# A two-layer transformer on one core: layer 1's attention weights loaded and padded when row 3's slot begins, in the tiles in which rows were prepared

## The chip, the core and the metric

The kernel runs on one core of a Trainium2 chip. A core has a matrix engine (TensorE, "PE" in the profile, its weight loads "PEld"), a vector engine (VectorE, "DVE"), an engine for activation functions (ScalarE, "ACT"), a general engine (GpSimd, "POOL") and a queue engine (SyncE, "SP") that issues most of the transfers. Each engine works through its own list of instructions in order and waits on semaphores for the others. The metric is the time of one execution in microseconds of device time; lower is better.

## The reference, cut to what matters

The input x is 4 rows (batch entries) of 512 tokens with 128 channels, all in 32-bit floats. Two layers are computed, each as x = x + attention(norm(x)) + experts(norm(x)):

```python
# layer 0: a window of 64 tokens per token and head, and 16 gated experts (best 4)
strain = disp_win - disp[:, :, :, None, :]
bond_logits = gelu(strain @ W_strain + rel_emb @ W_pos) @ W_bond
damage = sigmoid(gelu(strain @ W_dmg + b_dmg) @ W_dmg_out + b_dmg_out)
weights = softmax(where(mask, bond_logits - 10.0 * damage, -inf))
# layer 1: full attention with 16 heads of 8 channels, and 8 relu experts (best 2)
q, k, v = split(xn @ w_qkv, 3)
attn = softmax(q @ k.T / sqrt(128)) @ v @ w_out
```

What the change touches is `w_qkv`, a matrix of 128 x 384 that gives layer 1's queries, keys and values.

## The kernel before, in words

The rows go through layer 0 one after the other, in the loop `for b in range(B)` (L731). In row b's slot four kinds of work are woven together step by step (`weave`): the band logits of row b (`band_logits`, L555: VectorE subtracts shifted projections into tiles `z`, L572, ScalarE puts them through Gelu, L574 and L578, TensorE sums them, L586); the gated experts of row b (`gated_experts`, L659); the band values of row b-1 (`band_values`, L305 on); and layer 1's relu experts of earlier rows (`relu_experts`, L399, whose two products are L388 and L454, with a relu on ScalarE, L396, and an addition on POOL, L459). In the second half of a slot the next row is also prepared (`prepare`, L504): normalised into tile `xn`, transposed into `xnT`, and scaled by its root mean square in tile `sq`.

At the end of a row's band logits the exponentials `e` are formed from the logits on VectorE (L628), taken on ScalarE (L632) and stored to memory as `by_t` (L633). The band values read them back in another order, into tiles `f` (L312), transpose them on TensorE (L321), copy them to `g` (L322), store them as `by_s` (L327) and read them as `wb` (L339) for the products with the values (L353).

After the loop, layer 0's pools are closed and layer 1's are opened in their place. `full_attention` runs for all four rows, woven with the band values of row 3 and the remaining relu experts. Its order on TensorE is written out by hand: a list of steps, in each of which products of scores (L935) for maxima (L952, VectorE) and for exponentials (L959, ScalarE) alternate, chained so that they stay in this order, and the experts' products are chained behind them. Everything else is ordered ahead of time by a planner: it takes the instructions in the order of the program, or ahead of it by 4000 where the code says so, and places each when its inputs should be ready.

Queries and keys are made for groups of four heads. `w_qkv` holds 8 columns a head; a product needs each head at 32 columns, so the weights are first spread into `wqk`: POOL clears it (L765) and VectorE copies the 8 columns of each head into it, once for the queries and once for the keys (L767). A group's queries are a product into the bank `abank` (L823) and a copy to tile `q` on ScalarE (L827); its keys are L832 and L836, and go through the same bank. The values are L811, and L815 copies them into `vaug`.

Tiles lie in pools, which are stacked in each partition's memory in the order in which they are opened: `keep`, `small`, `chain`, `wp`, and then for layer 0 `prep` (xn, xnT, sq and wdT, one buffer each), `hold0`, `zp` (four tiles of 8,192 bytes a partition, which hold the `z` and also the `e`), `lp`, `ap`, `fp`. For layer 1 the pools `work` (q, k, the results of attention), `one` (w_qkv, w_out, wqk, vaug, nmax) and `ep` (exponentials) take the place of layer 0's, from where `prep` began. `nmax` is cleared by POOL (L777) before VectorE writes maxima into it, and `vaug` likewise (L775, L776).

Of the kernel before, what the change touches and what calls it, by code (L numbers as in the profile page):

```python
# [22 lines left out]
FP = mybir.dt.float32  # L23
# [6 lines left out]
B, T, C = 4, 512, 128  # L30
# [49 lines left out]
def woven(*tracks):  # L80


    live = [[g, n, 0] for g, n in tracks]
    while live:
        t = min(live, key=lambda v: (v[2] + 1) / v[1])
        t[2] += 1
        if next(t[0], "end") == "end" or t[2] == t[1]:
            live.remove(t)
        yield


def weave(*tracks):
    for _ in woven(*tracks):
        pass
# [3 lines left out]
def two_layers(ctx: ExitStack, tc: tile.TileContext, w: dict, consts: bass.AP, out: bass.AP):  # L98
    nc = tc.nc
# [7 lines left out]
    def bank():  # L107
        return ps_f.tile([P, 512], FP, tag="f", name="bank")
# [16 lines left out]
    def c_(name):  # L125
        return cst[:, offs[name][0]:offs[name][1]]
# [80 lines left out]
    def layernorm(b, dst, pin=False):  # L207

        mv = small.tile([P, TPB, 2], FP, tag="mv", name="mv")
        for i in range(TPB):  # L210
            st = small.tile([P, 6], FP, tag="st", name="st")
            ins = nc.vector.bn_stats(st, x1[:, b * TPB + i, :])
            if pin and not i:
                tc.keep_in_program_order(ins)
            nc.vector.bn_aggr(mv[:, i, :], st)
        rs = inv_sqrt(mv[:, :, 1], 1.0)
        for i in range(TPB):
            nc.vector.tensor_scalar(
                dst[:, i, :], x1[:, b * TPB + i, :], mv[:, i, 0:1], rs[:, i:i + 1],
                ALU.subtract, ALU.mult,  # L220
            )

    def inv_sqrt(src, scale):

        sd = small.tile([P, TPB], FP, tag="sd", name="sd")
        nc.scalar.activation(sd, src, AF.Sqrt, bias=eps, scale=scale)
        rs = small.tile([P, TPB], FP, tag="rs", name="rs")
        nc.vector.reciprocal(rs, sd)
        return rs

    def transposed(src):

        pt = bank()
        for i in range(TPB):
            nc.tensor.transpose(pt[:, i * P:(i + 1) * P], src[:, i, :], ident)
        return pt
# [44 lines left out]
    def add_rows(b, py):  # L281
        nc.vector.tensor_tensor(rows_of(b), rows_of(b), py, ALU.add)


    chain = ctx.enter_context(tc.tile_pool(name="chain", bufs=2))
    wp = ctx.enter_context(tc.tile_pool(name="wp", bufs=2))
    xT = keep.tile([C, B * T], FP, name="xT")


# [178 lines left out]


    with ExitStack() as l0:  # L470
        prep = l0.enter_context(tc.tile_pool(name="prep", bufs=1))
        hold = l0.enter_context(tc.tile_pool(name="hold0", bufs=2))
        zp = l0.enter_context(tc.tile_pool(name="zp", bufs=4))
        lp = l0.enter_context(tc.tile_pool(name="lp", bufs=1))
# [29 lines left out]
        def prepare(b):  # L504

            xn = prep.tile([P, TPB, C], FP, tag="xn", name="xn")
            layernorm(b, xn, b > 0)
            pt = transposed(xn)
            xnT = prep.tile([C, T], FP, tag="xnT", name="xnT")
            nc.scalar.copy(xnT, pt)  # L510
            yield
            proj = hold.tile([P, 2, 2, PADW], FP, tag="proj", name="proj")
            nc.gpsimd.memset(proj[:, :, :, 0:4], 0.0)
            for kind in (1, 0):
                for hg in range(2):
                    pp = bank()
                    nc.tensor.matmul(pp, merged[:, kind, hg, :], xnT, start=True, stop=True)
                    nc.scalar.copy(proj[:, kind, hg, 4:4 + T], pp)
            ready[b] = [proj]
            yield  # L520
            sq = prep.tile([P, TPB, C], FP, tag="sq", name="sq")
            nc.vector.tensor_tensor(sq, xn, xn, ALU.mult)
            ss = small.tile([P, TPB], FP, tag="ss", name="ss")
            nc.vector.tensor_reduce(ss, sq, AX.X, ALU.add)
            rr = inv_sqrt(ss, 1.0 / C)
            for i in range(TPB):
                nc.vector.tensor_scalar_mul(sq[:, i, :], xn[:, i, :], rr[:, i:i + 1])

            xb = x1[:, b * TPB:(b + 1) * TPB, :]
            nc.vector.tensor_tensor(xb, xb, xn, ALU.add)  # L530
            yield
            pt = transposed(sq)
            tT = hold.tile([C, T], FP, tag="tT", name="tT")
            nc.scalar.activation(tT, pt, AF.Identity, scale=scale0)
            pv = bank()
            for i in range(TPB):
                nc.tensor.matmul(pv[:, i * P:(i + 1) * P], xnT[:, i * P:(i + 1) * P], w_val, start=True, stop=True)
            valn = chain.tile([P, TPB, C], FP, tag="valn", name="valn")
            nc.scalar.copy(valn.rearrange("p t c -> p (t c)"), pv)
            pg = bank()  # L540
            for i in range(TPB):
                nc.tensor.matmul(pg[:, i * E0:(i + 1) * E0], tT[:, i * P:(i + 1) * P], gate_wT, start=True, stop=True)
            scores = small.tile([P, TPB, E0], FP, tag="scores0", name="scores0")
            nc.vector.tensor_tensor(
                scores, pg[:, :TPB * E0].rearrange("p (t e) -> p t e", e=E0),
                gate_b[:, None, :].to_broadcast([P, TPB, E0]), ALU.add,
            )
            yield
            route = small.tile([P, TPB, E0], FP, tag="route0", name="route0")
            routes(zp, "z", scores, E0, K0, c_("lt16"), route)  # L550
            rT = route_rows(hold, route, E0, route_d[0][b], LIMIT + 1.0)
            ready[b] += [valn, tT, rT]
            yield
# [105 lines left out]
        def gated_experts(b):  # L659
# [40 lines left out]
            finish(*late)  # L700
            add_rows(b, ya)

        preparation = prepare(0)
        for _ in range(2):
            next(preparation)
# [25 lines left out]
        for b in range(B):  # L731
            logits_b, gated_b = band_logits(b), gated_experts(b)
            if not b:
                weave((logits_b, 6), (preparation, 4))
            first = [(logits_b, 30 if b else 24), (gated_b, 7)]
            second = [(logits_b, 37), (gated_b, 10)]
            if b:
                first.append((band_values(b - 1, ready[b - 1][1]), 23))
                experts[b - 1] = relu_experts(b - 1)
                second.append((experts[b - 1], 22))  # L740
            if b > 1:
                first.append((experts[b - 2], 22))
            if b + 1 < B:
                second.append((prepare(b + 1), 6))
            weave(*first)
            weave(*second)
# [4 lines left out]
    one = ctx1.enter_context(tc.tile_pool(name="one", bufs=1))  # L751
# [4 lines left out]
    def abank():  # L756
        return ps_a.tile([P, T], FP, tag="a", name="abank")

    w_qkv = one.tile([C, 3 * C], FP, name="w_qkv")
    nc.sync.dma_start(out=w_qkv, in_=w["L1_attn_w_qkv"])  # L760
    w_out = one.tile([C, C], FP, name="w_out")
    nc.sync.dma_start(out=w_out, in_=w["L1_attn_w_out"])

    wqk = one.tile([C, 2, 4, 4, 32], FP, name="wqk")
    nc.gpsimd.memset(wqk, 0.0)  # L765
    for s in range(2):
        nc.vector.tensor_copy(  # L767
            wqk[:, s, :, :, 0:8].rearrange("c g h e -> c (g h) e"),
            w_qkv[:, s * C:(s + 1) * C].rearrange("c (h e) -> c h e", e=8),
        )  # L770

    vaug = [one.tile([P, TPB, H, 32], FP, name=f"vaug{i}") for i in range(2)]
    nmax = [one.tile([P, TPB, 4, 32], FP, name=f"nmax{i}") for i in range(2)]
# [8 lines left out]
    def full_attention():  # L782
# [37 lines left out]
        def queries(n):  # L820
            b, g = groups[n]
            pq = abank()
            nc.tensor.matmul(  # L823
                pq, wqk[:, 0, g].rearrange("c h e -> c (h e)"), xT[:, b * T:(b + 1) * T], start=True, stop=True
            )
            q[n] = work.tile([P, T], FP, tag="q", name="q")
            nc.scalar.copy(q[n], pq)  # L827

        def keys(n):
            b, g = groups[n]  # L830
            pk = abank()
            nc.tensor.matmul(  # L832
                pk, wqk[:, 1, g].rearrange("c h e -> c (h e)"), xT[:, b * T:(b + 1) * T], start=True, stop=True
            )
            k[n] = work.tile([P, T], FP, tag="k", name="k", bufs=3)
            nc.scalar.activation(k[n], pk, AF.Identity, bias=c_("ones8"))  # L836
# [72 lines left out]
        for n, (b, g) in enumerate(groups):  # L909
            t = m_step[8 * n]  # L910
# [7 lines left out]
            t = x_step[8 * n + 7]  # L918
# [87 lines left out]
```

## Time and profile before

| what | us |
|---|---|
| three runs | 1360.2, 1353.03, 1360.58 |
| their median | 1360.2 |
| the profiled execution's own time | 1354.64 |
| its span, first to last instruction | 1352.8 |
| busy: TensorE, VectorE, ScalarE, POOL | 1165.9, 1007.9, 1018.8, 87.3 |
| row 3's slot of layer 0, about | 693 to 917 |
| first score product of layer 1 (L935) | 933.13 |

The profile is one execution. Its rows give busy time, which is not the same as time on the path: an engine that is idle may cost nothing, and a short step may hold up everything. The chain of work that ended last is followed back from the last instruction, at each step to what released it. Timelines give the start, the length, the engine, the line and what ended the idle time ahead of an instruction. Windows give the busy time of each engine in a stretch, with the clock that TensorE was granted (1.00 is full) and how busy the transfer engines were.

### The profile page before, as it was taken

Reading aid. Unit: us, or ns where it says so; the run is one execution under the profiler, and the core shown is the slowest. Engines: PE = TensorE matmul, PEld = TensorE weight load, DVE = VectorE, ACT = ScalarE, POOL = GpSimd, SP = SyncE. Lnnn points to the kernel's source line nnn. Section 1 sums busy time; section 2 is a strip of 40 time slices with the busy share of each in tenths; the row PEclk is TensorE's granted clock in tenths of the full one; section 3 lists DMA queues with packets and bytes.
Section 4 is the critical chain, followed back from the end, with each engine's and each line's share of the span. In section 5 each row is a group of like instructions: output and inputs, shape, how many; then the busy total and the mean of one; then the engine's idle time right before and its main releaser. Section 6 shows DMA issues by size and latency. Waiting matters only on the chain. (4 is left out here: it accounts for less than half of the span.)

```text
span 1352.8 us, 17415 instructions
## 1 busy us (share of the span) xinstructions
PE 1165.9 (86%) x6763; PEld 448.1 (33%) x6763; DVE 1007.9 (75%) x1085; ACT 1018.8 (75%) x1159; POOL 87.3 (6%) x68
## 2 busy tenths in 40 slices
PE   5676976677899879988987998897999999999997
PEld 2122322133434323334332343343333334333332
DVE  4999998999878899997779999843544445544441
ACT  4899997989888899999879999863454445555454
POOL 2000000000001021100100300002000000000000
PEclk9798988888999979998998999996999989999999
DMA  8121211446223434721244463223333210010100
GB/s 273 49 75 50 77 53 67 129 101 158 70 59 81 164 94 123 188 65 61 80 154 99 125 156 100 73 67 133 94 94 78 54 41 25 27 36 24 47 24 8
DMA packets 168524, 117.61 MB, mean 87 GB/s; under 512 B 66621, under 2 KB 149274, under 8 KB 166906
## 3 DMA queue, kind: packets, MB, share of 16 engines
q1 hardware_dynamic: 166970, 109.77, 29.6%
q0 software_dynamic: 1184, 6.29, 1.2%
q8 instruction: 54, 0.88, 0.3%
q10 hardware_dynamic: 288, 0.43, 0.1%
q14 instruction: 28, 0.23, 0.1%
HBM read 89.00 MB, written 27.46 MB: 86 GB/s over the span
## 5 line engine op out<-in xcount | busy, mean ns | idle before, releaser
L572 DVE TENSOR_TENSOR z<-proj 128x2044 f32<-128x2044 f32 (+31 forms) x256 | 553.6, 2185 | 22.6 <-PE lbank L586 13.5
L586 PE MATMUL lbank<-z,place 128*32 128x504 f32 (+18 forms) x2048 | 294.5, 649 | 105.3 <-ACT z L578 61.1
L952 DVE TENSOR_REDUCE nmax<-score 128x2 f32<-128x1024 f32 x128 | 156.3, 1225 | 194.1 <-PE score L935 193.7
L578 ACT ACTIVATE z<-z,posb 128x1024 f32<-128x1024 f32 (+31 forms) x256 | 266.7, 1097 | 8.1 <-DVE z L572 6.3
L574 ACT ACTIVATE z<-z,brep 128x2048 f32<-128x2048 f32 (+31 forms) x128 | 241.6, 1904 | 8.1 <-DVE z L572 7.0
L959 ACT ACTIVATE ex<-score 128x1024 f32<-128x1024 f32 x128 | 130.3, 1023 | 138.9 <-PE score L935 138.9
L935 PE MATMUL score<-k,q 32*128 32x512 f32 x512 | 142.6, 668 | 6.5 <-DVE nmax L952 4.0
L388 PE MATMUL bank<-xT,ew 128*128 128x512 f32 x256 | 137.0, 627 | 6.9 <-DVE e L628 5.7
L935 PE MATMUL score<-qa,k 32*128 32x512 f32 x512 | 139.5, 647 | 2.0 <-ACT ex L959 1.4
L459 POOL TENSOR_TENSOR total<-total,part 128x512 f32<-128x512 f32 x32 | 73.0, 2280 | 1044.1 <-DVE part L458 1018.2
L396 ACT ACTIVATE h<-bank,cols 128x512 f32<-128x512 f32 x144 | 97.8, 685 | 49.5 <-PE bank L388 48.9
L454 PE MATMUL bank<-h,ew 128*128 128x512 f32 x256 | 132.2, 614 | 2.5 <-ACT h L396 2.5
L586 PEld LDWEIGHTS lbank<-z,place 128*32 128x32 f32 x2048 | 44.3, 113 | 263.7 <-ACT z L578 128.7
L675 PEld LDWEIGHTS accbank<-wT,lin 128*128 128x128 f32 x512 | 71.3, 204 | 64.5 <-issue 38.3
L675 PE MATMUL accbank<-wT,lin 128*128 128x128 f32 x512 | 82.7, 300 | 9.0 <-DVE lin L673 8.9
L686 PE MATMUL gbank<-tT,wT 128*128 128x512 f32 x128 | 71.7, 642 | 19.1 <-DMA wT<-wT_all 18.3
L852 PE MATMUL accbank<-ex,vaug 128*32 128x512 f32 x512 | 70.6, 617 | 0.2 <-ACT ex L959 0.2
L693 PE MATMUL gbank<-tT,wT 128*128 128x512 f32 x128 | 67.4, 608 | 0.0
L689 ACT ACTIVATE glu<-gbank,gbt 128x512 f32<-128x512 f32 x64 | 43.8, 685 | 29.2 <-PE gbank L686 28.6
L454 PEld LDWEIGHTS bank<-h,ew 128*128 128x128 f32 x256 | 44.2, 193 | 59.6 <-issue 47.6
L935 PEld LDWEIGHTS score<-k,q 32*128 32x128 f32 x512 | 38.8, 190 | 75.2 <-ACT ex L959 31.3
L388 PEld LDWEIGHTS bank<-xT,ew 128*128 128x128 f32 x256 | 41.8, 193 | 66.2 <-issue 44.8
(188 smaller groups left out, 1192.3 us busy)
## 6 DMA issues: line engine op xcount, KB each, us to landing
r<-route SPq DMA_DIRECT2D x96, 256.0 KB, 3.4
ew<-in_L_ffn_W SPq DMA_DIRECT2D x64, 256.0 KB, 2.8
wb<-by_s SPq DMA_DIRECT2D x32, 512.0 KB, 5.5
wT<-wT_all SPq DMA_DIRECT2D x48, 192.0 KB, 2.4
by_t<-e SPq DMA_DIRECT2D x8, 1024.0 KB, 4.8
f<-by_t SPq DMA_DIRECT2D x128, 64.0 KB, 3.0
by_s<-g SPq DMA_DIRECT2D x16, 512.0 KB, 4.2
wb<-by_s SPq DMA_DIRECT2D x24, 256.0 KB, 3.0
```

What stands on the lines that cost most here:

```text
L388: mm = nc.tensor.matmul(ph, wt[:, c * P:(c + 1) * P], xT[:, b * T:(b + 1) * T], start=True, stop=True)
L396: nc.scalar.activation(h, ph, AF.Relu, bias=bias[:, c:c + 1])
L454: nc.tensor.matmul(py, old[1][:, c, :], old[0][c], start=(c == 0), stop=(c == 3))
L459: nc.gpsimd.tensor_tensor(total, total, part, ALU.add)
L572: nc.vector.tensor_tensor(z[:, :, :, 0:n], seen, own, ALU.subtract)
L574: nc.scalar.activation(z[:, :, :, 0:n], z[:, :, :, 0:n], AF.Gelu, bias=b_dmg)
L578: last = nc.scalar.activation(z[:, dq, :, 0:n], z[:, dq, :, 0:n], AF.Gelu, bias=posb[:, j:j + 1])
L586: mm = nc.tensor.matmul(ps[q:q + 32, t0:T], place[:, kind, 3 - dd:35 - dd], z[:, dq, hg, 0:n], start=(dd == 0), stop=(dd == 3),)
L675: nc.tensor.matmul(ya[:, i * P:(i + 1) * P], lin[:, i * P:(i + 1) * P], wT[:, 2, :], start=False, stop=(e == E0 - 1 and i == TPB - 1),)
L935: mm = nc.tensor.matmul(ps[:, h - two, :], own[r, i * P:(i + 1) * P], seen[r, :], start=True, stop=True)
L952: freed.append(nc.vector.tensor_reduce(nmax[n % 2][:, i, two:two + 2, 8:9], ps, AX.X, ALU.max, negate=True))
L959: freed.append(nc.scalar.activation(ex[n, i][:, two:two + 2, :], ps, AF.Exp, scale=inv))
```

## The change

The pool `prep` is opened outside layer 0's block, at the same place in the stack, and so stays open in layer 1. When the slot of row 3 begins, a new function loads `w_qkv` into the tile `sq`, clears two tiles (`xn` for the queries, `xnT` for the keys, as large as half of the old `wqk` each) on POOL, and copies the heads' columns into them on VectorE. No later row is prepared in these tiles. At the start of layer 1 the load, the clearing and the copies are gone; the two tiles `w_qkv` and `wqk` are gone from the pool `one`. The products that read the weights (L811, L823, L832) read the new tiles. `w_out` is loaded where it was.

```diff
+    prep = ctx.enter_context(tc.tile_pool(name="prep", bufs=1))
...
     with ExitStack() as l0:
-        prep = l0.enter_context(tc.tile_pool(name="prep", bufs=1))
...
+        def attention_weights():
+            w_qkv = prep.tile([C, 4, C], FP, tag="sq", name="w_qkv").rearrange("c a e -> c (a e)")
+            nc.sync.dma_start(out=w_qkv[:, 0:3 * C], in_=w["L1_attn_w_qkv"])
+            wqk = [prep.tile([C, 4, 4, 32], FP, tag=t, name="wqk") for t in ("xn", "xnT")]
+            for s in range(2):
+                nc.gpsimd.memset(wqk[s], 0.0)
+                nc.vector.tensor_copy(
+                    wqk[s][:, :, :, 0:8].rearrange("c g h e -> c (g h) e"),
+                    w_qkv[:, s * C:(s + 1) * C].rearrange("c (h e) -> c h e", e=8),
+                )
+            return w_qkv, wqk
...
+            if b == B - 1:
+                w_qkv, wqk = attention_weights()
...
-    w_qkv = one.tile([C, 3 * C], FP, name="w_qkv")
-    nc.sync.dma_start(out=w_qkv, in_=w["L1_attn_w_qkv"])
     w_out = one.tile([C, C], FP, name="w_out")
     nc.sync.dma_start(out=w_out, in_=w["L1_attn_w_out"])
-
-    wqk = one.tile([C, 2, 4, 4, 32], FP, name="wqk")
-    nc.gpsimd.memset(wqk, 0.0)
-    for s in range(2):
-        nc.vector.tensor_copy(
-            wqk[:, s, :, :, 0:8].rearrange("c g h e -> c (g h) e"),
-            w_qkv[:, s * C:(s + 1) * C].rearrange("c (h e) -> c h e", e=8),
-        )
...
-                pq, wqk[:, 0, g].rearrange("c h e -> c (h e)"), xT[:, b * T:(b + 1) * T], start=True, stop=True
+                pq, wqk[0][:, g].rearrange("c h e -> c (h e)"), xT[:, b * T:(b + 1) * T], start=True, stop=True
...
-                pk, wqk[:, 1, g].rearrange("c h e -> c (h e)"), xT[:, b * T:(b + 1) * T], start=True, stop=True
+                pk, wqk[1][:, g].rearrange("c h e -> c (h e)"), xT[:, b * T:(b + 1) * T], start=True, stop=True
```

## The prediction

> **What bounds the kernel now.** I read the page first. TensorE is the busiest engine over the whole span, VectorE and ScalarE are about equal behind it; the slices show two stages, one up to about 917 us (layer 0, VectorE and ScalarE near full) and one after it (layer 1, TensorE near full).
>
> ```profile
> PE 1165.9 (86%) x6763; PEld 448.1 (33%) x6763; DVE 1007.9 (75%) x1085; ACT 1018.8 (75%) x1159; POOL 87.3 (6%) x68
> ```
>
> The edit sits in row 3's slot of layer 0 and at the seam, so I read the chain of work that ended last between 905 and 965 us (columns: start, length, what).
>
> ```profile
> 915.77 1.92 ACT e L632
> ...
> 917.71 7.27 DMA by_t<-e
> ...
> 925.04 2.34 DMA w_qkv<-in_L_attn_w_qkv
> ...
> 927.57 0.67 DVE wqk L767
> ...
> 928.29 1.33 PE abank L823 x2
> ...
> 929.64 0.59 ACT q L827
> ...
> 930.28 2.09 PE abank L832 x2
> ...
> 932.39 0.69 ACT k L836
> ...
> 933.13 2.16 PE score L935 x8
> ```
>
> Layer 1 starts in single file: the last store of layer 0's exponentials lands at 925.04; only then is w_qkv asked for; copies, queries and keys follow one by one, and the first scores come at 933.13, 8.09 us after the landing. Who waits meanwhile, from the timelines and from SyncE's own waits:
>
> ```profile
> SPq L760 <- DMA by_t<-e: 5.2, 1, 5.2
> 925.46 0.95 POOL L765 MEMSET wqk<- 128x1024 f32 x1 [7.77 <-DMA ew<-in_L_ffn_W]
> 927.57 0.73 DVE L767 COPY wqk<-w_qkv 128x128 f32<-128x128 f32 x2 [1.10 <-DMA w_qkv<-in_L_attn_w_qkv]
> 928.29 1.32 PE L823 MATMUL abank<-xT,wqk 128*128 128x512 f32 x2 [2.60 <-DVE wqk L767]
> 923.81 1.88 PE L454 MATMUL bank<-h,ew 128*128 128x512 f32 x4
> ```
>
> TensorE has layer 0's spare expert products until 925.69 and then stands 2.60 us. The windows (length, PE, PEld, DVE, ACT, POOL busy, granted clock, DMA) show the rest of the price: it works at half clock from about 931 to 945.
>
> ```profile
> 916.00:925.00 9.00, 9.00 (x17) 3.50 (x18) 0.34 (x1) 5.12 (x6) 1.27 (x1) 0.84 0.77 290
> 925.00:931.00 6.00, 2.73 (x5) 0.80 (x4) 1.42 (x3) 0.58 (x1) 5.54 (x6) 0.84 0.41 112
> 931.00:936.00 5.00, 4.22 (x14) 1.36 (x13) 0.67 (x1) 0.69 (x1) 1.40 (x3) 0.50 0.63 184
> 936.00:942.00 6.00, 5.32 (x16) 1.95 (x15) 4.42 (x5) 0.13 (x1) 0.00 (x0) 0.50 0.00 0
> 947.00:953.00 6.00, 5.37 (x27) 2.22 (x27) 3.38 (x3) 2.06 (x3) 0.00 (x0) 1.00 0.57 124
> ```
>
> **What still waits after the change.** The obvious reading is that w_qkv being early frees the whole seam, from about 911 us. I doubt it, because of the pools. L760 waited for the store of e, although w_qkv's own bytes were never part of e. By the sizes in the code, counted per partition from the start of prep: prep holds 6,656 bytes (three tiles of 2,048, wdT 512), hold0 reaches to 31,360, zp (z and e) to 64,128. Before, work (26,624 bytes) lies at 0 to 26,624, and w_qkv at 26,624 to 28,160, inside hold0. That it waited on a reader of zp shows that a new pool waits for every old pool it overlaps, as a whole. Before, work overlaps prep and hold0 alone, so q and k didn't have to wait for e. After, prep stays, work lies at 6,656 to 33,280 and reaches 1,920 bytes into zp. So L827, the first write into work, should inherit the wait for 925.04. The edit removes what lay behind that landing, not the landing.
>
> **Part by part.**
> Removed from the path: the w_qkv transfer (2.34 us), the two copies (0.67) and the query product (1.33). After: the query product needs only weights and xT; it goes before the landing, into the 3.81 us in which TensorE stood idle up to 915.89, at no cost; without that gap it costs its 1.06. At 925.05 q is copied (0.59), keys 925.68 to 927.01 (two products at the 1.33 of L823's pair; 2.09 at half clock, 1.06 at full), k 0.69, first scores at about 927.8 in place of 933.1. **Gain 5.4**, between 4.6 and 5.6.
> What is late next: the first maxima need nmax0 cleared. POOL's queue then begins with vaug0 (1.80) and nmax0 (0.67) at 925.05, done by 927.5; the scores end at 928.9 or later, so it is not the bound. Behind the waiting q copy on ScalarE stand only steps for experts; the last of the five relus of that stretch began at 924.01, so even if q were put one place ahead, 0.7 us of ScalarE moves. The f loads wait on SyncE for the same landing and get one issue less ahead of them (0.39). They land about 932.9; f's transposes (L321) ran at 944.30 and would come near 937.5, still covered.
> The clock: score groups took 2.09 us at half clock and 1.14 from 947 on. Three groups (933, 937, 942) alternate with VectorE's maxima, so full clock would save 3 x 0.95 = 2.9. Here a page of the Trainium skill speaks against me: "TensorE: Matmul & The Clock Gate", Part 1, says the clock is lost when TensorE is idle for a whole window of about 3.4 us. The longest gap between 916 and 947 is 2.60, so by the rule shortening gaps brings nothing; by the row the clock was at 0.50 with gaps of 2.60 and less, so the share of idle time matters, and that falls. I take half, **1.4**; ends 0 and 2.9.
>
> Added to row 3's slot: two memsets, two copies, one transfer. The slot:
>
> ```profile
> 693.00:917.00 224.00, 195.44 (x1168) 79.60 (x1169) 196.25 (x188) 198.46 (x213) 22.00 (x8) 0.96 0.40 110
> 683.15 0.63 DVE L604 SCALAR_TENSOR_TENSOR logits<-dmg,lbank 128x456 f32<-128x456 f32 x1 [2.93 <-PE lbank L586]
> 752.08 9.54 POOL L459 TENSOR_TENSOR total<-total,part 128x512 f32<-128x512 f32 x1 [37.83 <-DVE part L458]
> ```
>
> xn's last reader runs at 620, sq's and xnT's (transposes, value products) at about 655, some 35 us before the slot. So the transfer waits for nothing: one issue of 0.33 on SyncE ahead of that slot's wT and r8 loads, and 2.3 to land, with the transfer engines at 0.40. POOL is busy 22 of 224 us: two memsets of about 0.48 (half of L765's 0.95) hide in its waits. If they landed ahead of an addition into total, it would be 1 us late, and its next comes tens of us later. The two copies are the only ones on a full engine (VectorE 196 and ScalarE 198 of 224). Their row says 583 to 659 ns each, 0.73 together, but beside POOL's memset of vaug, which ended at 928.15; a 128x128 step without company (L527) takes 0.28. So 0.56 for both; 0 if they fall into gaps like the 2.93 before L604. Against it stands "SBUF — State Buffer", section "Who interferes with whom": a copy in its two-port form and a POOL instruction lock each other out for a whole instruction. By the row VectorE never loses (six subtractions went through while one addition was stretched to 9.54); by the rule one copy could wait out such an addition, 9.5 more. POOL is busy a tenth of the time, so I take the row: **cost 0.6**, ends 0 and 10. w_out stays where it was.
>
> **Sum.** -5.4 - 1.4 + 0.6 = -6.2 us. From 950 on the windows sum to 383 busy us of TensorE in 403, in an order written out by hand, so what the start gains should travel to the end. The profiled execution took 1354.6 (span 1352.8 and 1.8 around it): 1348.4. That execution is 5.6 under the median; the three runs and it average 1357.1, so I forecast 1351.
>
> **The rivals.**
> *The wait is by tile, or the planner starts q before the landing.* For it: work's first tiles touch no byte of zp. Against: L760. Queries and keys would be ready by about 916; at most 17 us, less the VectorE time of e (4.48 us to 915.7) and its clash with the maxima: some 12. **1345**, chance 0.12.
> *Nothing arrives.* Row 3's band values go by way of two trips to memory, and TensorE stands for the second: in 1060 to 1090 L353 waits 3.5 us for wb. L353 at 956.5 came without a wait but with about 1 us to spare (g copied until 946.9, then the store at 4.1 and the load at 4.15 that the chain shows at 1075 and 1079, the second load issued 0.5 later). If the planner puts f's transposes at the same distance from the landing and not from the scores, the gain is given back at L353. Also possible is that the new plan merely shuffles. **1357**, chance 0.15.
> *Slower.* The planner, whose idea of when w_qkv lands is not the chip's, puts the copies on VectorE ahead of row 2's last steps (maxima from 686.9, e at 689.2), while the transfer stands on SyncE behind an issue that waits for experts (issues at 676.0 and 679.4). VectorE then stands until 682 or, behind the next such issue (689.2), until 692, and e, ScalarE's exponentials and all of row 3's slot follow on two engines 88% busy. Price up to 10; it decides once the stop is longer than the 6.2 gained. **1364**, and more where the order of the whole slot suffers, chance 0.18. Against it: the tiles are free at 655 and SyncE has slots at 655 to 660.
>
> **How the numbers follow.** Forecast 0.55: 1351, with 1345 to 1357 from the ends of its terms and the spread of the runs (1353 to 1360.6). 1% is 13.6 us, about what a measurement of this kernel can tell from no change: faster is below 1346.6, slower above 1373.8. Faster: nearly the first rival's half of more and the forecast's lower end, 0.21. Slower: the long tail of the last rival, 0.11. Within 1%: 0.68. The range reaches from the first rival's better half to the last one's middle: 1338 to 1366.
>
> **What would show it.** L767 and the w_qkv transfer before 700 us; L823 before the store of e has landed; L827 within 0.1 us of that landing; the first L935 about 2.8 us after it, where it was 8.1; a granted clock above 0.5 in the 15 us that follow. Wrong if L827 starts earlier than the landing (first rival), if L353 shows new waits for wb (second), or if VectorE stands before L767 (third). What would upset the number most is a changed order in row 3's slot, which I can't see from here.

## The result, and the profile after

| | before | after |
|---|---|---|
| median of 8 runs, us | 1358.87 (1353.03 to 1361.23) | 1352.52 (1350.31 to 1357.24) |
| ratio, 95% interval | | 0.9958 (0.9937 to 0.9978) |
| profiled execution: own time, span | 1354.64, 1352.8 | 1357.24, 1355.4 |
| last store of `e` lands | 925.04 | 934.11 |
| first score product of layer 1, after that landing | 8.09 | 2.56 |

The changed kernel is 0.2 to 0.6% faster, some 6 us of 1359. That is inside the 1% which I called no change: a small gain, close to the forecast of 1351. Two executions in the later runs, one of the changed kernel (5449.2 us) and the profiled one in the second set of the version with `nmax0` (5746.52), took some four times as long: the ratios leave them out, and that profile is not read.

The two profiled executions say the opposite, and this has to be cleared first. The profiled one of the changed kernel is the slowest of its eight runs (of those that count, in its three later sets too: 1355.12, 1355.56 and 1355.23), and the engines' busy time is the same within 2 us:

```profile
PE 1167.5 (86%) x6763; PEld 448.0 (33%) x6763; DVE 1008.2 (74%) x1085; ACT 1019.6 (75%) x1159; POOL 85.4 (6%) x69
```

Its layer 0 ended 9.1 us later (934.11 for 925.04). The lag had begun by 415 us, while the first added step runs at 625, and 5.8 us were there by 650; it comes in steps where TensorE's products ran 1.06 us in place of 0.59. In other profiled executions of kernels with the same added work the landing lay between 923.7 and 935.9. So an absolute time at the seam says nothing about the edit, and the totals of the profiled executions show no gain; the unprofiled ones do. Why the profiled ones of this kernel come out slow stays open. From here on I count from the landing of the last `by_t<-e` (the first issue on SyncE that waited for it), and compare what follows.

The chain of work that ended last in the changed kernel (start, length, what; L838, L842, L941 and L958 are the L832, L836, L935 and L952 of before):

```profile
934.99 0.91 PE abank L838 x2
...
935.93 0.69 ACT k L842
936.67 1.15 PE score L941 x8
...
938.00 2.37 DVE nmax L958 x2
...
940.42 1.15 PE score L941 x8
```

Its timeline between 905 and 945 us shows the rest (in brackets the idle time ahead and its releaser):

```profile
920.99 1.02 PE L829 MATMUL abank<-xT,wqk 128*128 128x512 f32 x2
...
933.12 1.88 PE L455 MATMUL bank<-h,ew 128*128 128x512 f32 x4
...
934.11 0.33 SPq L776 DMA_DIRECT2D w_out<-in_L_attn_w_out  x1
934.13 0.58 ACT L833 COPY q<-abank 128x512 f32<-128x512 f32 x1
...
934.72 1.80 POOL L781 MEMSET vaug<- 128x2048 f32 x1 [7.95 <-ACT q L833]
936.46 0.52 POOL L783 MEMSET nmax<- 128x512 f32 x1
```

The query product (L829) ran 13 us ahead of the landing. Its result then lay in the bank until 934.13: the copy to `q` (L833) began 0.02 us after the store had landed. What followed took 2.56 us to the first scores, where it took 8.09.

The windows of the changed kernel (length, PE, PEld, DVE, ACT, POOL busy, granted clock, DMA) cover the same parts of the seam, 9 us later:

```profile
925.00:934.00 9.00, 9.00 (x17) 3.47 (x18) 0.41 (x1) 5.11 (x6) 1.27 (x1) 0.81 0.76 291
934.00:940.00 6.00, 4.12 (x21) 1.74 (x19) 2.69 (x3) 1.27 (x3) 5.28 (x7) 1.00 0.34 85
940.00:945.00 5.00, 3.19 (x18) 0.92 (x18) 3.32 (x4) 0.58 (x1) 0.62 (x1) 1.00 0.51 150
```

The granted clock behind the seam is 1.00, where it had been 0.50 for some 14 us; the score groups take 1.15 from the first on, and not 2.16.

Last, the added steps in the slot of row 3, on VectorE's timeline: 0.21 us each, between short steps, and VectorE then stands 1.35 us for ScalarE at 682.5.

```profile
681.54 0.21 DVE L711 COPY wqk<-w_qkv 128x128 f32<-128x128 f32 x1
...
682.28 0.21 DVE L711 COPY wqk<-w_qkv 128x128 f32<-128x128 f32 x1
```

### The profile page after: what moved, and what is told of

Read it like the earlier page. It is cut to its first block, busy times and chain, and to the rows that moved or that the text cites. A ratio compares the mean times of both kernels' runs of the same rounds, so it can differ in the third digit from the quotient of the medians.

```text
span 1355.4 us, 17417 instructions
## 1 busy us (share of the span) xinstructions
PE 1167.5 (86%) x6763; PEld 448.0 (33%) x6763; DVE 1008.2 (74%) x1085; ACT 1019.6 (75%) x1159; POOL 85.4 (6%) x69
## 5 line engine op out<-in xcount | busy, mean ns | idle before, releaser
L958 DVE TENSOR_REDUCE nmax<-score 128x2 f32<-128x1024 f32 x128 | 156.3, 1225 | 188.3 <-PE score L941 188.1
L941 PE MATMUL score<-k,q 32*128 32x512 f32 x512 | 139.4, 643 | 9.1 <-DVE nmax L958 6.5
L941 PE MATMUL score<-qa,k 32*128 32x512 f32 x512 | 139.1, 646 | 2.0 <-ACT ex L965 1.4
L941 PEld LDWEIGHTS score<-k,q 32*128 32x128 f32 x512 | 38.3, 185 | 76.6 <-ACT ex L965 31.2
```

What stands on the lines that cost most here:

```text
L941: mm = nc.tensor.matmul(ps[:, h - two, :], own[r, i * P:(i + 1) * P], seen[r, :], start=True, stop=True)
L958: freed.append(nc.vector.tensor_reduce(nmax[n % 2][:, i, two:two + 2, 8:9], ps, AX.X, ALU.max, negate=True))
```

## The experiments

The theory: (1) the landing stays the gate because `work` now reaches 1,920 bytes into `zp`, (2) 5.4 us of serial work behind it are gone, (3) the clock adds 1.4, and (4) the slot of row 3 pays 0.6. Each run below goes for one of these. Each ratio is to the kernel before on the same chip. The table gives us after the landing, each row from one profile; the versions of its last four rows come below:

| kernel | landing at | first scores | first exponentials | last product with row 3's `wb` | half-clock score groups |
|---|---|---|---|---|---|
| before | 925.04 | 8.09 | 34.17 | 171.67 | 3 |
| extra work only | 933.53 | 8.12 | 32.05 | 169.37 | 1 |
| the same again | 923.71 | 8.13 | 32.06 | 169.18 | 1 |
| load only | 926.51 | 5.16 | 28.14 | 165.47 | 0 |
| changed | 934.11 | 2.56 | 25.63 | 162.71 | 0 |
| changed again | 934.25 | 2.70 | 25.76 | 162.77 | 0 |
| changed, third | 935.86 | 2.56 | 25.62 | 161.62 | 0 |
| changed, fourth | 932.28 | 2.56 | 25.61 | 162.59 | 0 |
| gate taken away | 931.51 | -3.62 | 24.63 | 160.35 | 0 |
| the same again | 934.53 | -3.80 | 26.94 | 164.44 | 2 |
| next gate too | 929.02 | -3.99 | 22.02 | 160.87 | 0 |
| gap filled | 930.02 | 7.16 | 33.41 | 169.47 | 0 |

**The changed kernel again.** No edit.

> The changed kernel once more, for a second profile and more runs. Theory (only the seam changed; layer 0 is the same program but for two short copies): first score product 2.6 us after the last store of e lands (8.1 before), the part from that landing to layer 1's wait for wb (L354, near 1084) 149.8 us again, layer 0 up to the landing anywhere within 925 to 934 us, since most of the 9 us by which the changed kernel's profile was late there lie ahead of the first instruction that the change adds (5.8 at 650 us). Time 4 to 8 us below before. Rival (the change costs layer 0 some 3 to 9 us): the landing is again near 934 while a profile of the old order has it near 925.

> The changed kernel beside the two on the same chip, and a third profile of it. Theory: 5 to 7 us below before; first scores 2.6 us after the landing; full clock in the seam. Rival: none of its own; it tells whether the order after, narrow, maxima cleared early holds on one chip.

> The changed kernel as the measure for the two below, on one chip. Theory: ratio to before between 0.993 and 0.996.

Measured: 1351.36, ratio 0.9952 (0.9932 to 0.9973); 1348.95, 0.9928 (0.9904 to 0.9953); 1351.15, 0.9946 (0.9929 to 0.9962). With the first result that is four comparisons, all below 1; their mean, 0.9946, is 7.3 us. The second of these gained more than the 5 to 7 us that I had put down for it. What follows: the gain is there, and the four rows of the table repeat within 0.15 us up to the first exponentials.

**Extra work only.** Layer 0 as in the changed kernel, with the load, clearing and copies at the start of row 3's slot; nothing uses their result, and the seam is that of before. Against the changed kernel:

```diff
-                w_qkv, wqk = attention_weights()
+                attention_weights()
...
+    w_qkv = one.tile([C, 3 * C], FP, name="w_qkv")
+    nc.sync.dma_start(out=w_qkv, in_=w["L1_attn_w_qkv"])
+    wqk = one.tile([C, 2, 4, 4, 32], FP, name="wqk")
+    nc.gpsimd.memset(wqk, 0.0)
...
```

> The old seam, and in row 3's slot the early load, clearing and copies as extra work whose result nothing reads. Prices the added work alone. Theory: 0.2 us per copy on VectorE, hidden; time within 1 us of before, first scores 8.1 us after the landing. Rival (added work hurts the full stage: the copies or clearings shut out POOL or VectorE, the transfer delays the experts' loads): 3 to 10 us above before, with row 3's slot longer by that.

> The old seam with the early work as extra, once more, since its first interval (0.9987 to 1.0023) leaves open a cost of up to 3 us, and its profile had a layer 0 as late as the changed kernel's. Theory (the layer 0 of a profile is early or late by the clock that TensorE happened to be granted, not by the added work): ratio 1.000 again, and the landing may lie anywhere from 925 to 934. Rival (the added work costs about 3 us): 1.002 or more, landing near 933 again.

Measured: 1358.11, 1.0005 (0.9987 to 1.0023), and 1355.49, 0.9993 (0.9972 to 1.0014). What follows: the early steps cost nothing that can be measured (the intervals leave 3 to 4 us either way), and the open `prep` alone brings nothing; the gain is at the seam. Nor do they make layer 0 late: the second profile has the landing at 923.71, ahead of the kernel before. Row 3's first step into `xn` (L218), ahead of all the added work, already ran at 598.0 to 603.5 in the four profiles of the changed kernel, and at 594.52 before. From there to the landing they took 332.4 to 334.7 us; the kernel with the filled gap, which has no early work, took 334.0, and before 330.5. Both show the old chain behind the landing, 8.1 us again, but only one score group at half clock. In the chain of work of the first one:

```profile
933.53 2.40 DMA w_qkv<-in_L_attn_w_qkv
...
936.05 0.86 DVE wqk L783
...
941.65 2.16 PE score L951 x8
...
946.26 1.15 PE score L951 x8
```

**The load alone.** `w_qkv` comes early; clearing, copies and query product stay at the seam. Against the changed kernel:

```diff
-                w_qkv, wqk = attention_weights()
+                w_qkv = attention_weights()
...
+    wqk = [one.tile([C, 4, 4, 32], FP, name=f"wqk{s}") for s in range(2)]
+    for s in range(2):
+        nc.gpsimd.memset(wqk[s], 0.0)
+        nc.vector.tensor_copy(
+            wqk[s][:, :, :, 0:8].rearrange("c g h e -> c (g h) e"),
+            w_qkv[:, s * C:(s + 1) * C].rearrange("c (h e) -> c h e", e=8),
+        )
```

> Only the load of w_qkv is moved to row 3's slot; clearing and copying stay at the seam, in two tiles of their own. Theory (the serial steps behind the landing are the price, each with its own length): landing, clearing 0.5, copy 0.3, query product 1.1 to 1.3, q 0.6, keys 1.1 to 2.1, k 0.7: first scores 4.4 to 5.6 us after the landing; TensorE's gap shrinks from 2.6 to about 1 us and the clock may hold. Time 2.5 to 5.5 us below before. Rival (the transfer alone was the stall): 2.6 after the landing and the whole gain of the change. Rival (the half clock comes from the gap of 2.6 us): full clock here, so 5 us or more below before.

Measured: 1353.07, 0.9972 (0.9960 to 0.9984); the changed kernel beside it 0.9952. The chain of work, from the landing at 926.51:

```profile
926.77 0.53 POOL wqk L773
...
927.32 0.52 DVE wqk L774
...
927.88 1.14 PE abank L830 x2
...
929.09 0.59 ACT q L834
...
929.80 1.11 PE abank L839 x2
...
931.67 1.21 PE score L942 x8
```

What follows: taking out the transfer brings the first scores 2.9 us forward (8.09 to 5.16), of which 1.0 is the keys' products at full clock (1.11 for 2.09); the padding and the query product are worth another 2.6. TensorE's gaps up to the first scores are 0.5 and 0.8 us, and its products run at full clock from the landing on: here these shorter gaps kept the clock. The whole is 3.8 us by the ratio, under the 5 that I had expected if the clock held.

**The gate taken away.** The changed kernel with one buffer fewer in `work`, so that it ends 128 bytes short of `zp`:

```diff
-            oT = work.tile([C, T], FP, tag="oT1", name="oT1")
+            oT = work.tile([C, T], FP, tag="oT1", name="oT1", bufs=1)
```

> The changed kernel with one buffer for oT1 in place of two, so that the pool work ends 128 bytes short of zp. Theory (work waits for the store of e only because its range reaches into zp): q is copied, keys and the first scores are made before the landing, in TensorE's gap ahead of it; the first maxima then wait for nmax0, which is still cleared after the landing, at 2.4 us after it in place of 3.9. Time 1 to 4 us below the changed kernel, if the changed plan does not cost elsewhere. Rival (the wait is by tile, or the landing is not what held q): q starts where it does in the changed kernel, time the same.

> The narrow version again. Theory: first exponentials of layer 1 about 1 us earlier against row 3's first f load than in the changed kernel, 24.3 for 25.3, and 0.7 of that lost to a new wait for row 3's first wb; so 0.5 to 2 us below the changed kernel, at the edge of what the runs can tell. Rival (the changed plan of layer 1 gains by itself): 3 us or more below it.

Measured: 1349.46, 0.9944 (0.9922 to 0.9966), and 1349.12, 0.9937 (0.9916 to 0.9958). The timeline of the first:

```profile
919.52 0.58 ACT L833 COPY q<-abank 128x512 f32<-128x512 f32 x1 [4.87 <-PE abank L829]
...
927.89 1.14 PE L941 MATMUL score<-k,q 32*128 32x512 f32 x8
...
931.51 0.33 SPq L776 DMA_DIRECT2D w_out<-in_L_attn_w_out  x1
...
933.85 0.52 POOL L783 MEMSET nmax<- 128x512 f32 x1
934.41 2.36 DVE L958 TENSOR_REDUCE nmax<-score 128x2 f32<-128x1024 f32 x2 [11.57 <-POOL nmax L783]
```

What follows: in both profiles `q` is copied 12.0 us ahead of the landing, at 931.51 in the first, and the first scores run 3.6 to 3.8 ahead of it. So it was the reach of the pool that tied `q` to the store of `e`; no byte of `q` lay in `zp`. It gains little more, though: VectorE's maxima need `nmax` cleared, which lies in `one`, over `zp`, and so still waits for the landing; they start 2.90 after it, where they started 3.89. And the second profile lost the clock: TensorE stood 2.50 us for the maxima, two score groups ran at 2.09, and the first exponentials came at 26.94, later than in the changed kernel, which I had not expected. The first profile stood 2.31 at the same place and kept the clock. The ratio fell by 0.0008 and 0.0009 against the changed kernel on the same chip, some 1.2 us with overlapping intervals: in the right direction and not separated.

**The next gate taken away too.** The same, with `nmax0` in the lasting pool and cleared at the start:

```diff
+    nmax0 = keep.tile([P, TPB, 4, 32], FP, name="nmax0")
+    nc.gpsimd.memset(nmax0, 0.0)
...
-    nmax = [one.tile([P, TPB, 4, 32], FP, name=f"nmax{i}") for i in range(2)]
+    nmax = [nmax0, one.tile([P, TPB, 4, 32], FP, name="nmax1")]
```

> The narrow version, with the first of the two maxima tiles in the pool that is always open and cleared at the kernel's start. Theory (in the narrow version the first maxima stood 11.6 us for that clearing, which waits for the landing): maxima run ahead of the landing, on a VectorE that is idle there, and the first scores for exponentials come 2 to 5 us earlier against the landing; time 1 to 5 us below the narrow version, so 7 to 12 below before. Rival (the spare expert products are only pushed behind the scores, and TensorE is full either way; or row 3's f, g and wb become the wait): same as the narrow version within 1 us.

> The narrow version with the first maxima tile cleared early, again. Theory: first exponentials 3.6 us earlier than in the changed kernel, of which 2.3 go back to a new wait for row 3's first wb (seen in its first profile): 1 to 2.5 us below the changed kernel. Rival (nothing is given back): 3.5 us or more below it.

Measured: 1347.5, 0.9913 (0.9889 to 0.9936), and 1348.86, 0.9923 (0.9897 to 0.9949). In the first one's profile the maxima begin 2.81 us ahead of the landing at 929.02, from the chain of work:

```profile
925.10 1.08 PE score L944 x8
...
926.21 2.37 DVE nmax L961 x2
...
939.62 4.95 DMA by_s<-g
944.59 3.96 DMA wb<-by_s
948.68 0.63 PE bank L356 x12
```

Here row 3's band values do take back a part of what the start gains: TensorE stands for the first `wb` as well as for the second. The waits of TensorE between 925 and 1100 us (sum, count, longest), where the changed kernel had one of 3.5:

```profile
PE bank L356 <- DMA wb<-by_s: 5.8, 2, 3.5
```

The first exponentials come at 22.02, 3.6 us earlier than in the changed kernel; the last `wb` product comes at 160.87, 1.5 earlier than the mean of the four profiles of the changed kernel (162.4). Some 2.1 were given back, about what the waits grew by (5.8 less 3.5). It has the lowest median on both of its chips, on the one by only 0.26 us below the version with one gate gone; against the changed kernel on the same chip it is 0.0015 and 0.0023 lower, again with overlapping intervals.

**The gap filled.** The kernel before, with five products that nobody reads chained behind an expert product, so that TensorE has work while the old seam waits (against the kernel before):

```diff
-                    nc.tensor.matmul(py, old[1][:, c, :], old[0][c], start=(c == 0), stop=(c == 3))
+                    spare.append(nc.tensor.matmul(py, old[1][:, c, :], old[0][c], start=(c == 0), stop=(c == 3)))
+                    if len(spare) == SEAM:
+                        idle = accbank()
+                        for _ in range(5):
+                            mm = nc.tensor.matmul(idle, ident, xT[:, 0:T], start=True, stop=True)
...
```

> The old order, with five products into an unused bank laid into TensorE's gap of 2.6 us between the last spare expert product and the query product; nothing reads them. Asks whether that gap is what brings the half clock. If it is (theory, after the run in which only the load was moved kept full clock over gaps of 0.5 and 0.8 us): the first score groups take 1.14 us in place of 2.09, granted clock near 1.0 from 931 us on, first scores 7 to 7.5 us after the landing (keys 1.1 in place of 2.09), and the time is 1 to 4 us below before if the shifted plan costs nothing. Rival (no idle shorter than a window of about 3.4 us loses the clock, so the half clock has another cause, such as the shorter idle stretches that follow): clock still 0.5 between 931 and 945, time within 1 us of before or above it.

Measured: 1358.32, 1.0005 (0.9993 to 1.0017). TensorE's timeline, and its windows:

```profile
929.28 1.88 PE L455 MATMUL bank<-h,ew 128*128 128x512 f32 x4
931.00 2.74 PE L459 MATMUL accbank<-xT,cst 128*128 128x512 f32 x6
...
933.57 1.02 PE L833 MATMUL abank<-xT,wqk 128*128 128x512 f32 x2
...
935.29 1.11 PE L842 MATMUL abank<-xT,wqk 128*128 128x512 f32 x2
...
937.18 1.14 PE L945 MATMUL score<-k,q 32*128 32x512 f32 x8
```

```profile
925.00:931.00 6.00, 6.00 (x15) 2.30 (x14) 0.00 (x0) 2.18 (x4) 0.56 (x1) 1.00 0.79 312
931.00:936.00 5.00, 5.00 (x13) 2.19 (x12) 1.38 (x3) 0.59 (x1) 5.00 (x6) 1.00 0.48 132
```

What follows: with the 2.6 us filled the clock stays at 1.00 and the scores take 1.14, so in this execution the idle stretch was what took the clock. But nothing of the 1 to 4 us that I had expected arrived. The fillers led to another plan behind the seam, in which row 3's first `wb` comes too late, and after that stop TensorE ran at a granted clock of 0.50 all the same:

```profile
955.38 0.78 PE L353 MATMUL bank<-wb,va 128*32 128x128 f32 x16 [2.38 <-DMA wb<-by_s]
```

```profile
955.75:959.16 3.41, 3.41 (x22) 1.02 (x11) 0.04 (x1) 0.00 (x0) 0.00 (x0) 0.50 0.96 224
```

So the first exponentials come 26.3 us after the first scores, where the changed kernel has 23.1 and the extra-work kernels 23.9, and the last `wb` product comes at 169.47, as in the extra-work kernels. What the clock at the seam is worth this run doesn't say.

## Why the prediction was right, point by point

**The landing stays the gate: right.** `q` begins 0.02 us after the landing, and 12 us before it once `work` ends short of `zp`. The first rival, queries and keys ahead of the landing, is false for this edit. Even where the gate was removed the ratios show about 1 us, not separated from none, and not 12, since the clearing of `nmax` was next.

**Removed from behind the landing, 5.4: right.** 8.09 less 2.56 is 5.5 (2.56 to 2.70 in four profiles); predicted start 2.8 after the landing. Some 4.5 of it are the steps that left; 1.0 is the clock again, as the keys' products took 1.06 for 2.09, where I had counted 1.33. `nmax0` was done 2.87 after it (predicted 2.5), and the maxima came at 3.89 behind the scores, so it was not the bound, as said. The transposes of `f` came at 11.0 after it for 12.5 predicted, covered either way.

**The clock, 1.4: right that it holds; what it brings is argued, and the half that I took was a guess.** What lies between the first scores and the last `wb` product took 163.6 us before, 161.3 and 161.1 in the extra-work kernels, and 159.1 to 160.2, mean 159.8, in the changed one. So 3.8 us went in the execution with three half-clock groups, and 1.4 and 1.2 in the two with one. That fits 2.9 and 1.0 of slower groups with something left, but the plans differ too, and no run changed the clock alone. In the profiles read here the price differs by what the execution granted, and the half that I took is near its lower cases.

The length of the slow stretch follows a grid that none of my terms had. In all twelve traces read, the granted clock changes only at steps of 3.41 us, whose place differs between executions. Before, a step with 0.81 us of products was followed by five at half clock; in the first extra-work profile one with 1.13 was followed by two:

```profile
925.68:929.09 3.41, 0.81 (x3) 0.30 (x2) 1.42 (x3) 0.00 (x0) 3.41 (x5) 1.00 0.49 137
929.09:946.16 17.07, 14.66 (x46) 6.19 (x46) 7.07 (x7) 2.44 (x4) 3.31 (x4) 0.50 0.23 66
```

```profile
935.31:938.72 3.41, 1.13 (x2) 0.30 (x2) 1.01 (x3) 0.56 (x1) 3.41 (x4) 1.00 0.46 122
938.72:945.54 6.82, 5.96 (x18) 2.80 (x18) 1.70 (x2) 0.71 (x2) 2.35 (x4) 0.50 0.53 145
```

The Trainium skill, "TensorE: Matmul & The Clock Gate", Part 1, would have given no gain, for no gap reached its 3.4 us window; but half clock followed gaps of 2.60, 2.34 and 2.45, each with two of 0.7 to 0.8 behind it, and the filled gap and the load-only kernel had none there. This chain of TensorE is of the second extra-work profile:

```profile
922.82 1.88 PE L455 MATMUL bank<-h,ew 128*128 128x512 f32 x4
...
927.15 1.13 PE L839 MATMUL abank<-xT,wqk 128*128 128x512 f32 x2 [2.45 <-DVE wqk L783]
...
928.99 2.08 PE L848 MATMUL abank<-xT,wqk 128*128 128x512 f32 x2 [0.72 <-ACT q L843]
...
931.85 2.09 PE L951 MATMUL score<-k,q 32*128 32x512 f32 x8 [0.78 <-ACT k L852]
```

My own reason, that the share of idle time matters, is not borne out as a rule either. The first profile with the gate taken away stood 2.31, 1.38 and 1.39 us within 10 us and kept full clock; the second lost it after 2.50. Their emptiest steps are nearly alike, 1.53 and 1.62 us of products:

```profile
933.07:936.48 3.41, 1.53 (x8) 0.70 (x7) 2.07 (x2) 0.00 (x0) 3.41 (x5) 1.00 0.38 97
```

```profile
938.15:941.56 3.41, 1.62 (x10) 0.64 (x10) 3.29 (x5) 0.00 (x0) 2.21 (x4) 1.00 0.39 103
```

**The slot, 0.6: none that can be measured.** 1.0005 and 0.9993 for the extra work alone. The copies took 0.21 each, not 0.28, and VectorE stood for ScalarE right behind them.

**"By the row VectorE never loses": wrong, without harm here.** That sentence chose the low end for the slot. The copies at the old seam refute it: in the four profiles with that seam (before, twice extra work, gap filled), each pair ended 0.08 to 0.15 us after POOL's clearing of the first `vaug` did (before: clearing to 928.15, copies to 928.23 and 928.30), the first copy having begun 0.54 to 0.77 ahead of that end. The load-only kernel has the plainest case, on POOL's and VectorE's timelines:

```profile
927.69 1.88 POOL L782 MEMSET vaug<- 128x2048 f32 x1
...
928.07 1.58 DVE L774 COPY wqk<-w_qkv 128x128 f32<-128x128 f32 x1
```

The copy of 0.21 us took 1.58 and ended 0.08 after the clearing. That is what the Trainium skill, "SBUF — State Buffer", section "Who interferes with whom", says of a copy in its two-port form and a POOL instruction, and the rule that I set aside for the row. In the slot no POOL instruction lay beside the copies, so its 10 never came due; at the seam the edit gained by it instead: of the 0.67 us of copies that left the chain, some 0.25 (0.67 less two of 0.21) was this wait.

**The gain reaches the end: right.** The last `wb` product came 170.1 us after the landing on the mean of the first three profiles with the old seam (169.5 with the gap filled) and 162.4 on that of the changed kernel's four, 7.7 apart. From there to the end of the span all took about 256.1 to 256.3, but for two of the changed profiles at 258.6, in which a few products near 1139 us ran at half clock. The runs say 7.3. The second rival, that `wb` takes it back, is false for this edit: L354 waits 3.5 us for `wb` near 1083 as L353 did. It came true in part for the versions with gates taken away, where TensorE's waits for `wb` sum to 4.2 to 5.8 us, and for the filled gap (5.8). The third, copies that block VectorE, is false: VectorE doesn't wait ahead of them, and the extra-work kernels are level with before.

**What was luck.** The forecast summed to 6.2 us of gain for a measured 7.3, with one term too low, as it seems (the clock), and one too high (the slot), and the level that it started from, 1357.1, was 1.8 below the median measured beside the change. And what I called the greatest danger, a changed order in row 3's slot, simply did not come; nothing in the prediction had shown that it would not.

## What to carry to other kernels

A load, a padding or a product that hangs behind the last landing of a stage should leave it whenever its target memory can outlive the stage; what it brings is the chain behind that landing, and removing a link shows the next (here the pool's reach, then the clearing of `nmax`, then `wb`). Who waits is decided by a pool's whole range, not by the bytes of a tile, so here the copy into one that reached 1,920 bytes into an old pool waited for the landing, and the copy into one that ended 128 bytes short ran 12 us ahead of it. Where an early stage varies by more than the edit is worth, measure in the trace from an event that both kernels share, and leave the total to many runs.

## What the runs showed of the hardware that I had not expected

TensorE's clock fell to half after 2.3 to 2.6 us without work in four of the profiles, with nearly the same gaps it held in one, and it changed only at steps of 3.41 us: half clock behind the seam lasted five of them before (17.07 us) and two in both extra-work executions. A VectorE copy of 0.21 us took 0.51 to 1.58 beside a clearing on POOL, and ended 0.08 to 0.15 after it in ten of ten cases. And a layer 0 with the same work in it ended between 923.7 and 935.9 us, more than the whole edit is worth; where I followed it, the lag came with products of TensorE at a lower granted clock.
